# Four partition quarters of the softmax denominators: added through small DMAs and VectorE instead of a product on TensorE

## The chip, the cores and the metric

The kernel runs on one core of one Trainium2 chip. The metric is device time in microseconds (us) of one execution; lower is better. Before the change it is 1316.64 us, the median of three runs (1314.28, 1316.64, 1318.42).

## What is computed

One transformer block in fp32, on an input x of 2 x 512 tokens of width 512, cut to what matters here:

```python
x = x + layernorm(attention(layernorm(x)))   # 32 heads of 128
x = x + layernorm(ffn(layernorm(x)))         # dense base + 8 gated experts of rank 16

# attention, per batch b and head h (64 pairs):
attn = softmax(q[b, h] @ k[b, h].T / sqrt(128))    # 512 x 512
out  = attn @ v[b, h]                              # 512 x 128
# then all heads side by side, 4096 wide:  out @ Wo + bo
```

q and k carry an RMS norm over all 4096 columns and a gain. The change concerns one step of the softmax: the sum of the exponentials of each query, by which the output is divided.

## The kernel before, in words

**Stages.** After the first layer norm the kernel computes q and k (to about 405 us of the profiled span) and then a first part of v; everything is parked in device memory. Products of weights use Winograd's form of 2x2 block products with seven products in place of eight, so that sums of operands are formed on VectorE and GpSimd. From about 450 us to 1232 us runs the **attention loop** (L714 to L762 and the lines after it), and then a tail with the rest of the output product, two layer norms and the feed-forward part.

**The attention loop.** It has N = 64 turns, turn i being head i // 2 of batch i % 2. The order of the instructions on TensorE (PE), VectorE (DVE), ScalarE (ACT) and GpSimd (POOL) is exactly the order in which the program emits them; only the order of the DMAs in the queue of SyncE (SP) is laid out by the framework's scheduler. An engine never runs past an instruction that waits. In turn i:

- DVE: `sums(i - 1)` (L546): the exponentials of the turn before, laid out as keys on partitions and queries along the free axis, are added with a 32x32 block transpose on the way (L550), then over the four blocks of keys (L557). The result, `part`, holds 16 columns for each of 128 partitions: partition 32a + r holds the sum over the a-th quarter of the partitions for query r of each block of 32. So the four quarters still have to be added.
- DVE: `below_top(i)` (L577) subtracts the maximum, 128 x 2048 elements.
- PE: `scores(i + 1)` (L531), four products; ACT copies each out (L532). Then ACT takes the exponential of turn i in one instruction (L580).
- In every even turn: `reciprocals` (L559) for the two turns before. PE multiplies `part` by `same`, a constant 0/1 matrix with a one wherever two partitions are equal modulo 32 (L563). This adds the quarters and leaves the sum in all four. DVE takes the reciprocal from PSUM (L567), and for each of the two turns spreads it out (L570) and multiplies the output with it (`divided`, L598); ACT adds the bias of v (L599).
- PE: the fill. These are steps of v (L460; 1 or 2 a turn up to turn 43, more before turn 8) and tasks of the output product (`through_wo`, L646): group g of eight turns has 14 tasks, and they run in turns 8(g+1) to 8(g+1)+7, for g = 0 to 5. A v step and a task each take 1.72 us of PE. Line L697 deals the tasks out: turns 0 to 7 of a group get 2, 2, 2, 1, 2, 2, 2, 1. From turn 57 on each turn has one `outward` product (L690) of 3.44 us in their place; turn 56 has none.
- DVE: `top_of(i + 1)` (L541, L542) takes the maximum of the next turn's scores over keys, and POOL brings it together over the partitions (L544). Every second turn has two sums of heads on DVE (`head_sums`, L619 to L625), and the turns from 56 on the combining of the output product (L680). Then the results of the fill leave PSUM, through DVE or ACT.
- PE: `weighted(i)` (L589): the product of the exponentials with v. It waits for the exponential of this turn, and for `divided(i - 2)`, because the outputs have two PSUM banks.

Results of v steps, tasks and the product with `same` take turns in three PSUM banks called aux; `bank()` (L515) lets the earlier result leave before a bank is used again. Weights of the output product are loaded by `load_right` (L635) into two buffers.

Of the kernel before, what the change touches and what calls it, by code (L numbers as in the profile page):

```python
# [9 lines left out]
F32 = mybir.dt.float32  # L10
AF = mybir.ActivationFunctionType
ALU = mybir.AluOpType
AX = mybir.AxisListType

P = 128
# [4 lines left out]
NT = S // P  # L20
# [12 lines left out]
def kernel(ctx: ExitStack, tc: tile.TileContext, x, wq, wk, wv, wo, vecs, rows, wbase, gates, bexp, out):  # L33
# [11 lines left out]
    nc = tc.nc  # L45
    B = x.shape[0]
    N = H * B
# [15 lines left out]
    small = ctx.enter_context(tc.tile_pool(name="small", bufs=4))  # L63
# [3 lines left out]
    def tt(name):  # L67
        return tmp.tile([P, 512], F32, tag="tmp", name=name)
# [41 lines left out]
    same = const.tile([P, 4, 32], F32, tag="same", name="same")  # L110
# [196 lines left out]
    def attention():  # L307
# [6 lines left out]
        G = GH * B  # L314
# [23 lines left out]
        WG = NG - 2  # L338
# [52 lines left out]
        for i in range(2):  # L391
            of, to = (v.rearrange("p (g j) -> p g j", j=GH) for v in (vec[:, i, :], steps[:, i, :]))
# [33 lines left out]
        def load_wo(g):  # L426
            wos[g] = []
            for k in range(2):
                w = hpool.tile([P, 2, 512], F32, tag="h", name=f"wo{g}_{k}")
                nc.sync.dma_start(out=w, in_=wo[ts(2 * g + k, 2 * P), :].rearrange("(j p) f -> p j f", p=P))  # L430
                wos[g] += [w[:, j, :] for j in range(2)]
# [60 lines left out]
        def fetch_v(b, c):  # L492

            v = vpool.tile([P, NT, 256], F32, tag="v", name=f"v{b}_{c}")
            src = keptv[b, c // 2].rearrange("t p f -> p t f")
            nc.sync.dma_start(out=v, in_=src[:, :, ts(c % 2, 256)])
            vs[b, c] = v
# [3 lines left out]
        def fetch(i):  # L501
            h, b = divmod(i, B)
            k = kpool.tile([P, 512], F32, tag="k", name=f"kh{b}_{h}")
            nc.sync.dma_start(out=k, in_=keptk[b, h])
            q = qpool.tile([P, 512], F32, tag="q", name=f"qh{b}_{h}")
            nc.sync.dma_start(out=q, in_=keptqs[b, h])
            qs[i], kk[i] = q, k
# [7 lines left out]
        def bank(tag):  # L515
            tile = banks[tag].pop(0)
            banks[tag].append(tile)
            while any(of is tile for of, _ in pending):
                pending.pop(0)[1]()
            return tile  # L520
# [25 lines left out]
        def sums(i, part):  # L546


            quarters = small.tile([P, NT, 16], F32, tag="quarters", name=f"quarters{i}")
            nc.vector.tensor_reduce(  # L550
                quarters.rearrange("p k j -> p (k j)"),
                ss[i].rearrange("p k (j r) -> p (k j) r", r=32),
                AX.X,
                ALU.add,
                apply_transpose=True,
            )
            nc.vector.tensor_reduce(part, quarters.rearrange("p k j -> p j k"), AX.X, ALU.add)  # L557

        def reciprocals(turns, part):  # L559

            n = len(turns)
            psd = bank("aux")[:, 0 : n * 16]
            nc.tensor.matmul(  # L563
                psd, same.rearrange("p i c -> p (i c)"), part.rearrange("p n j -> p (n j)"), start=True, stop=True
            )
            inv = small.tile([P, 2, 16], F32, tag="inv", name=f"inv{turns[0]}")[:, 0:n]
            nc.vector.reciprocal(inv.rearrange("p n j -> p (n j)"), psd)  # L567
            for k, i in enumerate(turns):
                r = tt(f"r{i}")
                nc.vector.transpose(  # L570
                    r.rearrange("p (j c) -> p j c", c=32), inv[:, k].unsqueeze(2).to_broadcast([P, 16, 32])
                )
                yield i, r
# [5 lines left out]
        def exponentials(i):  # L579
            nc.scalar.activation(ss[i], ss[i], AF.Exp)  # L580
# [13 lines left out]
        def divided(i, r):  # L594
            h, b = divmod(i, B)
            po = pos.pop(i)
            o = opool.tile([P, 512], F32, tag="o", name=f"oh{b}_{h}")
            nc.vector.tensor_tensor(o, po, r, ALU.mult)  # L598
            nc.scalar.activation(o, o, AF.Identity, bias=bv[:, h : h + 1], scale=1.0)  # L599
            os[b, h] = o  # L600
            if (b, h % 2) != (1, 0):
                left_of[{(0, 0): 1, (0, 1): 2, (1, 1): 4}[b, h % 2], h // 2] = o
# [28 lines left out]
        def load_right(g, n):  # L631

            w = gpool.tile([P, 2, 512], F32, tag="g", name=f"wr{g}_{n}")
            for half, i in enumerate(product_order[2 * n : 2 * n + 2]):
                k, e = {1: (0, 0), 2: (1, 0), 3: (1, 1), 4: (1, 0), 5: (0, 0), 6: (1, 1), 7: (0, 1)}[i]  # L635
                src = (woq if i <= 3 else keptwo)[g, k]
                nc.sync.dma_start(out=w[:, half, :].rearrange("p (j f) -> p j f", j=2), in_=src[:, :, ts(e, 256)])
                right_of[i, g] = w[:, half, :].rearrange("p (j f) -> p j f", j=2)

        def through_wo(g, i, u):  # L640

            ps = bank("aux").rearrange("p (t e) -> p t e", t=2)
            for t in range(2):
                for j in range(2):
                    a = left_of[i, 2 * g + j][:, ts(2 * u + t, P)]
                    nc.tensor.matmul(ps[:, t, :], a, right_of[i, g][:, j, :], start=(j == 0), stop=(j == 1))  # L646
            to = acc[i][u]

            def add():
                if g > 0:  # L650
                    new = upool.tile([P, 512], F32, tag="u", name=f"w{i}_{g}_{u}").rearrange("p (t e) -> p t e", t=2)
                    nc.scalar.copy(new, ps)
                    nc.gpsimd.dma_start(out=to, in_=new, accum_op=ALU.add)
                elif i in bias_of:
                    nc.vector.tensor_tensor(to, ps, bias_of[i].unsqueeze(1).to_broadcast([P, 2, 256]), ALU.add)
                else:
                    nc.scalar.copy(to, ps)

            return add
# [34 lines left out]
        wo_tasks = {i: [] for i in range(N + 1)}  # L694
        for g in range(WG):
            for k in range(14):
                wo_tasks[G * (g + 1) + k * G // 14].append(  # L697
                    lambda g=g, k=k: through_wo(g, product_order[k // 2], k % 2)
                )
        last = N - G  # L700
# [19 lines left out]
        for i in range(N):  # L720
            g, n = divmod(i, G)
            if i + 3 < N:
                fetch(i + 3)
            c, n4 = divmod(i, 2 * B)
            if 2 <= n4 and 0 < c < H // 2 - 1:
                fetch_v(n4 - 2, c + 1)
            if g >= WG and n == 6:
                load_wo(g)
            if g < WG and n == 7:
                for k in range(2):  # L730
                    load_right(g, k)
            if 0 < g <= WG and n in (2, 4):
                load_right(g - 1, 1 + n // 2)
            if n == 0 and g > WG:
                combining = [step for u in range(2) for step in combined(u)]
            if i % 2 == 1:
                part = small.tile([P, 2, 16], F32, tag="part", name=f"part{i}")
            if i > 0:
                sums(i - 1, part[:, (i - 1) % 2])
            below_top(i)  # L740
            if i + 1 < N:
                scores(i + 1)
            exponentials(i)
            if i > 0 and i % 2 == 0 or i == N - 1:
                turns = (i - 2, i - 1) if i % 2 == 0 else (i - 1,)
                for turn, r in reciprocals(turns, part[:, 0 : len(turns)]):
                    divided(turn, r)
            want = 28 * (i + 1) // G if i < G else 28 + 56 * (i + 1 - G) // (5 * G - 4)
            while left and 84 - left < want:
                leaves(next(v_steps))  # L750
                left -= 1
            for task in wo_tasks[i]:
                leaves(task())
            top_of(i + 1)
            if n4 == 1:
                of_pair = head_sums(c - 1)
            if n4 % 2 == 1 and 0 < c <= 2 * WG:
                next(of_pair)
            for _ in range(3):
                if combining:  # L760
                    combining.pop(0)()
            while len(pending) > (len(wo_tasks[i]) if i >= last else 0):  # L762
                pending.pop(0)[1]()
            weighted(i)
        for task in wo_tasks[N]:
            leaves(task())
        sums(N - 1, part[:, 1])
        while pending:
            pending.pop(0)[1]()
        for turn, r in reciprocals((N - 1,), part[:, 1:2]):  # L770
            divided(turn, r)
        again = [[kpool.tile([P, 512], F32, tag="k", name=f"xr{b}_{t}") for t in range(NT)] for b in range(B)]
        for b in range(B):
# [206 lines left out]
```

## Time and profile before

| what | value |
|---|---|
| median of the runs | 1316.64 us (1314.28 to 1318.42) |
| the profiled execution: time | 1319.28 us |
| the profiled execution: span of the trace | 1317.4 us |
| PE busy | 1284.2 us, 97% of the span |
| DVE busy | 974.4 us, 74% |
| ACT busy | 534.8 us, 41% |
| POOL busy | 483.9 us, 37% |
| products with `same` (L563) | 33 of two passes each |
| granted clock of TensorE | 0.996 of full speed |

How to read it: the span runs from the first to the last instruction of one execution, and the execution's own time is 1.9 us more. The share of busy time is a mean over stages. The views that are used below are the page's groups of instructions (busy time, then mean duration in ns, then the idle time before), the waits (engine and line, what it waited for, total us, times, longest), and the timeline (start, duration, engine, line, operation, and in square brackets the idle time before it and what ended it). PE makes each fp32 product in two passes; an instruction's successor can start before its shown end, so costs are read from starts.

### The profile page before, as it was taken

Reading aid. Unit: us, or ns where it says so; the run is one execution under the profiler, and the core shown is the slowest. Engines: PE = TensorE matmul, PEld = TensorE weight load, DVE = VectorE, ACT = ScalarE, POOL = GpSimd, SP = SyncE. Lnnn points to the kernel's source line nnn. Section 1 sums busy time; section 2 is a strip of 40 time slices with the busy share of each in tenths; the row PEclk is TensorE's granted clock in tenths of the full one; section 3 lists DMA queues with packets and bytes.
Section 4 is the critical chain, followed back from the end, with each engine's and each line's share of the span. In section 5 each row is a group of like instructions: output and inputs, shape, how many; then the busy total and the mean of one; then the engine's idle time right before and its main releaser. Section 6 shows DMA issues by size and latency. Waiting matters only on the chain.

```text
span 1317.4 us, 11573 instructions
## 1 busy us (share of the span) xinstructions
PE 1284.2 (97%) x3470; PEld 643.5 (49%) x3470; DVE 974.4 (74%) x1204; ACT 534.8 (41%) x732; POOL 483.9 (37%) x368
## 2 busy tenths in 40 slices
PE   7999999999989999999999999999999999999997
PEld 4444444444434444455555555555555555434453
DVE  7565654888555468888788787878778888799575
ACT  5222222322221144344545445455454665545253
POOL 4789897565763011111122231322322333221002
PEclk9999999999999999999999999999999999999999
DMA  7789978598897765533366566566567565510001
GB/s 289 263 315 308 338 269 283 193 346 297 304 323 271 251 198 184 176 128 128 128 174 175 138 195 164 132 196 168 159 165 195 129 164 130 136 64 24 18 23 64
DMA packets 146127, 250.45 MB, mean 190 GB/s; under 512 B 11792, under 2 KB 39568, under 8 KB 146064
## 3 DMA queue, kind: packets, MB, share of 16 engines
q1 hardware_dynamic: 135120, 229.78, 51.3%
q0 software_dynamic: 10080, 18.35, 8.5%
q10 hardware_dynamic: 864, 1.57, 0.3%
q8 instruction: 28, 0.46, 0.1%
q14 instruction: 35, 0.29, 0.1%
HBM read 147.43 MB, written 83.89 MB: 176 GB/s over the span
## 4 chain that ended last, share of the span: by engine, by line
PE 64%; DVE 5%; ACT 2%; issue 0%; ACTq 0%; DVEq 0%
PE ps L531 16%; PE o L589 15%; PE aux L460 15%; PE aux L646 11%; PE psy L690 2%; PE p_k L217 2%; PE f L859 1%; ACT s L580 1%; DVE quarters L550 1%; DVE s L577 1%; PE hg L852 1%; PE f L915 1%; DVE m L541 0%; DVE y L680 0%; DVE oh L598 0%
## 5 line engine op out<-in xcount | busy, mean ns | idle before, releaser
L544 POOL PARTITION_ALL_REDUCE top<-m x64 | 122.6, 1916 | 620.7 <-DVE m L542 620.7
L532 ACT ACTIVATE s<-ps,rk 128x512 f32<-128x512 f32 x256 | 175.8, 687 | 312.4 <-PE ps L531 306.8
L589 PE MATMUL o<-s,v 128*128 128x512 f32 x512 | 231.0, 594 | 9.3 <-ACT s L580 9.3
L531 PE MATMUL ps<-qh,kh 128*128 128x512 f32 x512 | 230.2, 592 | 0.0
L531 PEld LDWEIGHTS ps<-qh,kh 128*128 128x128 f32 x512 | 97.3, 190 | 122.5 <-issue 121.7
L589 PEld LDWEIGHTS o<-s,v 128*128 128x128 f32 x512 | 96.6, 190 | 113.4 <-issue 96.4
L550 DVE TRANSPOSE_TENSOR_REDUCE quarters<-s 128x64 f32<-128x2048 f32 x64 | 147.1, 2299 | 0.0
L577 DVE TENSOR_TENSOR s<-s,top 128x2048 f32<-128x2048 f32 x64 | 146.0, 2281 | 0.0
L580 ACT ACTIVATE s<-s 128x2048 f32<-128x2048 f32 x64 | 121.7, 1902 | 12.9 <-DVE s L577 12.8
L541 DVE TENSOR_TENSOR m<-s 128x1024 f32<-128x1024 f32 x64 | 78.0, 1218 | 57.9 <-ACT s L532 57.9
L460 PE MATMUL aux<-w_v,t 128*128 128x512 f32 x256 | 115.8, 596 | 0.0
L237 ACT ACTIVATE sq_q<-q 128x512 f32<-128x512 f32 x62 | 38.9, 631 | 137.0 <-DVE q L290 68.3
L237 ACT ACTIVATE sq_k<-k 128x512 f32<-128x512 f32 x62 | 38.6, 630 | 137.1 <-DVE k L290 64.6
L238 POOL TENSOR_TENSOR accq<-accq,sq_q 128x512 f32<-128x512 f32 x62 | 81.0, 1310 | 36.2 <-ACT sq_q L237 29.3
L238 POOL TENSOR_TENSOR acck<-acck,sq_k 128x512 f32<-128x512 f32 x62 | 86.2, 1395 | 20.3 <-ACT sq_k L237 17.2
L646 PE MATMUL aux<-wr,oh 128*128 128x256 f32 x384 | 88.1, 380 | 0.0
L460 PE MATMUL aux<-w_v,nT_a 128*128 128x512 f32 x192 | 87.5, 596 | 0.0
L217 PE MATMUL p_k<-t,s_k 128*128 128x512 f32 x192 | 85.0, 592 | 0.0
L217 PE MATMUL p_q<-t,s_q 128*128 128x512 f32 x192 | 85.0, 592 | 0.0
L646 PEld LDWEIGHTS aux<-wr,oh 128*128 128x128 f32 x384 | 72.7, 190 | 20.8 <-issue 12.0
L460 PEld LDWEIGHTS aux<-w_v,t 128*128 128x128 f32 x256 | 47.6, 190 | 55.0 <-issue 54.3
L468 DVE TENSOR_TENSOR o_v<-aux,u_v 128x512 f32<-128x512 f32 x64 | 43.5, 684 | 41.4 <-PE aux L460 34.5
(185 smaller groups left out, 1733.8 us busy)
## 6 DMA issues: line engine op xcount, KB each, us to landing
keptq<-q SPq DMA_DIRECT2D x64, 256.0 KB, 7.0
q<-keptq SPq DMA_DIRECT2D x16, 1024.0 KB, 6.7
w_v<-keptw SPq DMA_DIRECT2D x32, 512.0 KB, 3.9
keptk<-k SPq DMA_DIRECT2D x64, 256.0 KB, 6.7
keptqs<-q SPq DMA_DIRECT2D x64, 256.0 KB, 7.0
qh<-keptqs SPq DMA_DIRECT2D x64, 256.0 KB, 2.9
kh<-keptk SPq DMA_DIRECT2D x64, 256.0 KB, 2.7
keptv<-o_v SPq DMA_DIRECT2D x64, 256.0 KB, 3.0
```

The lines of the kernel that those rows point to most:

```text
L217: nc.tensor.matmul(ps, a[:, c, ts(j, P)], x[c], start=(c == 0), stop=(c == 1))
L238: nc.gpsimd.tensor_tensor(accs[b], accs[b], sq, ALU.add)
L460: nc.tensor.matmul(ps, x[c][:, ts(t, P)], w[:, c, :], start=(c == 0), stop=(c == 1))
L531: nc.tensor.matmul(ps, kk[i][:, ts(k, P)], qs[i], start=True, stop=True)
L532: nc.scalar.activation(s[:, k, :], ps, AF.Copy, scale=rks[b][:, k : k + 1])
L541: nc.vector.tensor_tensor(m, s[:, 0:2, :], s[:, 2:4, :], ALU.max)
L544: nc.gpsimd.partition_all_reduce(ms[i], m[:, 0, :], P, ReduceOp.max)
L550: nc.vector.tensor_reduce(quarters.rearrange("p k j -> p (k j)"), ss[i].rearrange("p k (j r) -> p (k j) r", r=32), AX.X, ALU.add, apply_tr ...
L577: nc.vector.tensor_tensor(s, s, top.unsqueeze(1).to_broadcast([P, NT, 512]), ALU.subtract)
L580: nc.scalar.activation(ss[i], ss[i], AF.Exp)
L589: nc.tensor.matmul(po, vs[b, c][:, k, ts(j, P)], ss[i][:, k, :], start=(k == 0), stop=(k == NT - 1))
L646: nc.tensor.matmul(ps[:, t, :], a, right_of[i, g][:, j, :], start=(j == 0), stop=(j == 1))
```

## The change

The product with `same` goes. In its place `spread` (new) copies `part` from SBUF to SBUF on SP's queue, so that each quarter of the partitions gets the sums of the other three beside its own: for each of three rotations two DMAs, since a rotation wraps around, six in all, each of 32, 64 or 96 partitions by 128 bytes. DVE then adds the four (a `tensor_reduce` of 128 x 32 outputs from 128 x 128 inputs) and takes the reciprocal in SBUF.

So that the copies can travel, `reciprocals` and `divided` are emitted later in the turn, after the v steps. The tasks of the output product are dealt out as 0, 2, 2, 2, 2, 2, 2, 2 over the eight turns of a group, and two of its loads are issued one turn later. `part` is larger and has three buffers in place of four; `quarters` has one in place of four. `same` itself stays, for the identity matrix.

```diff
@@ sums
-            quarters = small.tile([P, NT, 16], F32, tag="quarters", name=f"quarters{i}")
+            quarters = small.tile([P, NT, 16], F32, tag="quarters", name=f"quarters{i}", bufs=1)
@@
-        def reciprocals(turns, part):
+        def spread(n, four):
+
+            for k in range(1, 4):
+                for to, of, m in ((0, k, 4 - k), (4 - k, 0, k)):
+                    nc.sync.dma_start(
+                        out=four[32 * to : 32 * (to + m), k, 0:n], in_=four[32 * of : 32 * (of + m), 0, 0:n]
+                    )
+
+        def reciprocals(turns, four):
 
             n = len(turns)
-            psd = bank("aux")[:, 0 : n * 16]
-            nc.tensor.matmul(
-                psd, same.rearrange("p i c -> p (i c)"), part.rearrange("p n j -> p (n j)"), start=True, stop=True
+            inv = small.tile([P, 2, 16], F32, tag="inv", name=f"inv{turns[0]}")[:, 0:n]
+            nc.vector.tensor_reduce(
+                inv.rearrange("p n j -> p (n j)"), four.rearrange("p a n j -> p (n j) a"), AX.X, ALU.add
             )
-            inv = small.tile([P, 2, 16], F32, tag="inv", name=f"inv{turns[0]}")[:, 0:n]
-            nc.vector.reciprocal(inv.rearrange("p n j -> p (n j)"), psd)
+            nc.vector.reciprocal(inv.rearrange("p n j -> p (n j)"), inv.rearrange("p n j -> p (n j)"))
@@ tasks of the output product
-                wo_tasks[G * (g + 1) + k * G // 14].append(
+                wo_tasks[G * (g + 1) + 1 + k // 2].append(
@@ the loop
-            if 0 < g <= WG and n in (2, 4):
-                load_right(g - 1, 1 + n // 2)
+            if 0 < g <= WG and n in (3, 5):
+                load_right(g - 1, (n + 1) // 2)
...
             if i % 2 == 1:
-                part = small.tile([P, 2, 16], F32, tag="part", name=f"part{i}")
+                part = small.tile([P, 4, 2, 16], F32, tag="part", name=f"part{i}", bufs=3)
             if i > 0:
-                sums(i - 1, part[:, (i - 1) % 2])
+                sums(i - 1, part[:, 0, (i - 1) % 2])
+            turns = ()
+            if i > 0 and i % 2 == 0 or i == N - 1:
+                turns = (i - 2, i - 1) if i % 2 == 0 else (i - 1,)
+                spread(len(turns), part)
+                four = part[:, :, 0 : len(turns)]
             below_top(i)
             if i + 1 < N:
                 scores(i + 1)
             exponentials(i)
-            if i > 0 and i % 2 == 0 or i == N - 1:
-                turns = (i - 2, i - 1) if i % 2 == 0 else (i - 1,)
-                for turn, r in reciprocals(turns, part[:, 0 : len(turns)]):
-                    divided(turn, r)
             want = 28 * (i + 1) // G if i < G else 28 + 56 * (i + 1 - G) // (5 * G - 4)
             while left and 84 - left < want:
                 leaves(next(v_steps))
                 left -= 1
+            if turns:
+                for turn, r in reciprocals(turns, four):
+                    divided(turn, r)
             for task in wo_tasks[i]:
                 leaves(task())
@@ after the loop
-        sums(N - 1, part[:, 1])
+        last_part = small.tile([P, 4, 2, 16], F32, tag="part", name="last_part", bufs=3)
+        sums(N - 1, last_part[:, 0, 0])
+        spread(1, last_part)
         while pending:
             pending.pop(0)[1]()
-        for turn, r in reciprocals((N - 1,), part[:, 1:2]):
+        for turn, r in reciprocals((N - 1,), last_part[:, :, 0:1]):
             divided(turn, r)
```

## The prediction

> **What bounds the kernel.** I read the page's busy times first, then the waits, then the timeline of PE and DVE through the attention loop.
>
> ```profile
> PE 1284.2 (97%) x3470; PEld 643.5 (49%) x3470; DVE 974.4 (74%) x1204; ACT 534.8 (41%) x732; POOL 483.9 (37%) x368
> ...
> DVE inv L567 <- PE aux L563: 44.6, 28, 3.9
> ...
> PE o L589 <- ACT s L580: 9.3, 8, 2.4
> ```
>
> PE is the bound. The busy times by stretch show no idle PE at all from 487 to 1010 us (523.00 of 523.00), 2.6 us from 1010 to 1145 and 8.0 us from 1145 to 1232. So in the loop up to turn 46 whatever leaves PE is won, as long as no new wait appears. The second row says that DVE already waits for the product that goes, 28 times, 1.6 us each on average: a DMA wait in its place is no loss until it is longer. The third row is the few waits of PE for the exponential, all from turn 47 on. The timeline of PE shows the price of the product and one of these waits:
>
> ```profile
> 1029.31 3.60 PE L531 MATMUL ps<-qh,kh 128*128 128x512 f32 x8
> 1032.74 3.62 PE L646 MATMUL aux<-wr,s_o 128*128 128x256 f32 x16
> 1036.19 3.60 PE L589 MATMUL o<-s,v 128*128 128x512 f32 x8
> 1039.63 3.60 PE L531 MATMUL ps<-qh,kh 128*128 128x512 f32 x8
> 1043.06 0.30 PE L563 MATMUL aux<-part,same 128*128 128x32 f32 x2
> 1043.20 3.70 PE L646 MATMUL aux<-wr,s_o 128*128 128x256 f32 x16
> 1046.74 3.60 PE L589 MATMUL o<-s,v 128*128 128x512 f32 x8
> 1050.17 3.60 PE L531 MATMUL ps<-qh,kh 128*128 128x512 f32 x8
> 1053.61 1.89 PE L646 MATMUL aux<-wr,s_o 128*128 128x256 f32 x8
> 1056.35 3.70 PE L589 MATMUL o<-s,v 128*128 128x512 f32 x8 [0.85 <-ACT s L580]
> ```
>
> Turns 45, 46 and 47. Without the product, tasks plus scores take 1036.19 - 1029.31 = 6.88; with it 1046.74 - 1039.63 = 7.11. Turn 47 has one task, and PE stands 0.85 for the exponential.
>
> **The product goes.** 0.14 between starts (1043.06 to 1043.20) and 0.09 that the next products take longer (3.54 against 3.45): 0.23 us each. In turns 2 to 54, 27 products at 0.23 = **-6.2**. The six after that stand where PE waits anyway: 0 (bound -1.4). The Trainium skill, "TensorE: Matmul & The Clock Gate", section "Wait — 56ns, not 53.3ns?", puts the floor of a small matmul at about 25 ns from start to start; two passes would be 0.05 and the gain an estimated 1.4 in place of 6.2. These starts disagree, and I go by them.
>
> **The tasks move.** Turns 47, 51 and 55 get a second task, so their waits (0.85, 0.86, 0.86 in the timeline) go: **-2.6**. Turns 8, 16, ... 48 get none. PE needs about 2.8 us between scores and `weighted` to cover copy and exponential (turn 47: 1056.35 - 1053.61 = 2.74). Turns 16, 24 and 40 keep two v steps (3.44): covered. Turn 32 keeps one: it waits like turn 47, 0.86. Turn 48 keeps nothing, like turn 56 today, which waits 2.44. Turn 8 keeps one and is taken up below. The shifted loads keep their two turns of lead: no cost.
>
> **The new wait, D: from the end of `part` to the last copy landed.** No row shows a small copy. SP issues six in a row; kh and qh start 0.38 apart (1063.51, 1063.89), the shortest issue is 0.32, three kh together take 1.44 (0.48 each). I take five steps of 0.40. The smallest landings: 2.0 for a 256 KB store, 2.4 for a 256 KB load (kh), 3.3 for a 512 KB one (v). So 256 KB cost about 0.9, and nothing but overhead is 1.1 (store) or 1.5 (load); I take 1.4, nearer the load since it must be seen in SBUF. D = 2.0 + 1.4 + 0.05 = **3.45**. Ends: 5 x 0.32 + 1.1 = 2.7; 5 x 0.48 + 2.4 = 4.8, and 5.5 if they queue behind other loads. The Trainium skill, "DMA: Bandwidth & Descriptors", section "Anatomy of one DMA — SWDGE (gpsimd) path", gives every DMA about 2.0 us of fixed cost, and its rules for authors advise against transfers under 64 KB. With 2.0 for 1.4 the sum below would rise by an estimated 2 to 3 us, to about no change.
>
> ```profile
> 1058.45 2.30 DVE L550 TRANSPOSE_TENSOR_REDUCE quarters<-s 128x64 f32<-128x2048 f32 x1
> 1060.78 0.26 DVE L557 TENSOR_REDUCE part<-quarters 128x16 f32<-128x64 f32 x1
> 1060.96 2.28 DVE L577 TENSOR_TENSOR s<-s,top 128x2048 f32<-128x2048 f32 x1
> 1063.66 0.36 DVE L567 RECIPROCAL inv<-aux 128x32 f32<-128x32 f32 x1 [0.42 <-PE aux L563]
> 1064.05 0.71 DVE L570 STREAM_TRANSPOSE r<-inv 128x512 f32<-128x512 f32 x1
> 1064.80 0.69 DVE L598 TENSOR_TENSOR oh<-o,r 128x512 f32<-128x512 f32 x1
> ```
>
> Turn 48: `part` ends at 1061.04 and L577 covers 2.2 of D; DVE then waits D - 2.2 = 1.25. The added reduce reads twice L557's elements: 0.26 to 0.36 by L557 and L567, next start about 0.24 later. The reciprocal I leave at 0.39 (PSUM or SBUF, +-0.05). Behind the waiting reduce on DVE stand both transposes, both `divided`, the next maximum (and POOL's after it), and exits of v steps.
>
> *Does DVE become the bound?* From L567 of turn 48 (1063.66) to that of turn 50 (1084.52) DVE idles 1.38 + 1.03, so it works 18.45; after, 18.69 + 1.25 = 19.94. PE needs 6 x 3.44 = 20.64 for the pair. Covered; break-even at D = 2.2 + 20.64 - 18.69 = **4.15**. While v steps run, DVE has 3.8 (turn 12) to 5 us (turn 32) idle a pair: covered to D of about 5.5.
>
> *Turn 8.* `part` ends at 564.35 by the timeline; + 3.45 + 0.24 + 0.39 + 0.75 + 0.69 = 569.87. PE would want `weighted` at 562.63 + 3.43 + 1.72 = 567.78: it waits 2.1 for `divided(6)`. Turn 48: without turn 47's wait `part` ends 0.87 earlier against PE, the same sum gives 5.8 after the scores began, before the exponential (6.1): 2.44 stands. New waits together 2.44 + 0.86 + 2.1 = **+5.4**.
>
> *Turns 56 to 63.* DVE is full here, and PE's waits follow it. DVE waits today at turns 56, 58, 60, 62, 63: 2.47, 0.23, 0, 2.19, 0 = 4.9; after, five times 1.25 + 0.24 = 7.45. +2.5 if all of it counts, 0 if the shorter waits at 56 and 62 give it back into PE's gaps (1.61 in turn 57). I take **+1.0** (ends 0 and +4.5, the three new waits alone).
>
> *SP's queue.* 198 DMAs more at about 0.35. The copies wait at its head for `part`; kh, qh and v behind them are due two or more turns later: 0. The last spread stands behind a load of Wo that waits for PE (1230.24 today), lands near 1234.5, and is needed only by the second half of the final product, after 1245: 0. One-buffer `quarters` stays on one engine: 0.
>
> **Sum:** -6.2 - 2.6 + 5.4 + 1.0 = **-2.4**. The profiled execution (span 1317.4, time 1319.28) would take 1316.9; the median of the runs lies 2.64 lower, so I forecast **1314.2**.
>
> **Rivals.**
> *The copies land sooner (D = 2.7).* For it: bytes are almost none. Turn 8 waits 1.35; turns 56 to 63 have five times 0.74 = 3.7 in place of 4.9, -1.2. Sum -6.2 - 2.6 + 4.65 - 1.2 = -5.3: **1311.3**. Bottom of the range 1308, with the last products' 1.4 and some scatter of the runs.
> *DVE becomes the bound (slower).* Place: turns 46 to 63; decides from D = 4.15. At D = 4.8: five pairs x 0.65 = 3.3; turn 8 +1.35; turn 48 now waits for `divided(46)`, +1.0; the three new waits of the last turns 3 x 1.35 = 4.0. Sum -2.4 + 9.7 = +7.3: **1323.9**. At D = 5.5, +1.35 a pair: about +15, 1332. For it: loads of 256 KB land at 2.7 to 2.9 by the median and DMA is 58% busy; against: in the late loop little is in flight when `part` ends.
> *It doesn't do what it says:* PE loses the products but idles as much. That is the first case with a turn or two more uncovered, within 2 us of no change.
>
> **Chances.** Forecast 0.37, early landing 0.30, DVE bound 0.33. The range 1308 to 1329 reaches into both rivals. About 0.3% (4 us) is what a measurement of this kernel can tell from no change: faster by more 0.31, within 0.36, slower 0.33; the forecast's own range is 1312 to 1319.
>
> **What would show it.** L563 gone, tasks plus scores 6.88 in every turn; PE waits new at 8, 32 and 48 and gone at 47, 51, 55; `part` to reduce 3.45; DVE idle near 1.25 before the reduce. Wrong if a copy's issue or landing is far from 0.40 and 1.4, or if v steps' exits behind the reduce hold PE's banks.

## The result and the profile after

The changed kernel takes **1354.76 us** (median of 4 runs, 1350.44 to 1357.23), the kernel before 1317.53 us on the same chip: ratio **1.0272** [1.0248, 1.0296]. It is 36 us slower. The forecast was 1314.2 with a range of 1308 to 1329, so it is wrong in sign and outside its range. The way it went is the slower rival, *DVE becomes the bound*, but at more than twice the price that the rival had at its far end (+15).

The page of the changed kernel, busy times, then the chain that ended last by engine, then the group of the new reduce (busy, mean ns, idle time before it and what ended that):

```profile
PE 1293.7 (96%) x3404; PEld 639.2 (47%) x3404; DVE 985.6 (73%) x1237; ACT 538.9 (40%) x732; POOL 484.0 (36%) x368
...
PE 63%; DVE 21%; DMA 5%; SPq 4%; issue 3%; ACT 2%; POOL 2%; DVEq 0%; ACTq 0%; POOLq 0%
...
L571 DVE TENSOR_REDUCE inv<-part 128x32 f32<-128x128 f32 (+1 forms) x32 | 12.0, 374 | 103.2 <-DMA part<-part 103.2
```

The chain on the page before:

```profile
PE 64%; DVE 5%; ACT 2%; issue 0%; ACTq 0%; DVEq 0%
```

DVE is busy 73% of the span, as before (74%), so the share of busy time shows nothing. The chain does: DVE has 21% of it where the page before has 5%, and two new members stand beside it, SP's queue (4%) and the DMA of `part` (3%). (The chain before reaches back only to 380 us, so its shares add up to 71%. From turn 1 to turn 63 alone, DVE has 255 of the chain's 781 us after the change, and 56 of 744 before.) The third line of the changed kernel is the cause in one row: DVE stands still 103.2 us ahead of 32 reduces, 3.2 us each, until the copies have landed. Before, it stood 44.6 us for the product in the same place. PE has 66 instructions fewer and is yet busy 9.5 us longer; that is a second effect, taken up below.

The row of the copies and their landing, from the view of the tile `part` (duration of one issue, min/median/max ns; then the time from issue to landing):

```profile
L563 SPq DMA_DIRECT2D part<-part x192: 522/589/1487, 480.5 to 1257.0; - x192
...
DMA to landing us min/median/max: 1.7/1.8/4.6
```

An issue takes 0.59 us by the median where the prediction took 0.40, and a landing 1.8 where it took 1.4. Turn 48 in the timeline of all engines, the same place as the rows of DVE in the prediction:

```profile
1076.14 3.60 PE L531 MATMUL ps<-qh,kh 128*128 128x512 f32 x8
1076.43 0.26 DVE L557 TENSOR_REDUCE part<-quarters 128x16 f32<-128x64 f32 x1
1076.61 2.28 DVE L584 TENSOR_TENSOR s<-s,top 128x2048 f32<-128x2048 f32 x1
1076.72 4.38 SPq L563 DMA_DIRECT2D part<-part  x6
...
1082.56 0.37 DVE L571 TENSOR_REDUCE inv<-part 128x32 f32<-128x128 f32 x1 [3.67 <-DMA part<-part]
1082.96 0.35 DVE L574 RECIPROCAL inv<-inv 128x32 f32<-128x32 f32 x1
...
1084.16 0.69 DVE L605 TENSOR_TENSOR oh<-o,r 128x512 f32<-128x512 f32 x1
...
1084.95 5.37 PE L596 MATMUL o<-s,v 128*128 128x512 f32 x8 [5.21 <-issue]
```

`part` ends at 1076.69. Six issues take 4.38 us, 0.73 each, and the reduce starts at 1082.56: D = 5.87 in place of 3.45. L584 covers the first 2.2, and the remaining 3.67 is DVE's idle time. `weighted` waits for `divided` (L605), so PE stands 5.21 us. Then comes something the prediction had no term for: the same eight passes take 5.37 us, not 3.67.

The busy times by stretch for turns 1 to 8, 8 to 46, 46 to 56 and 56 to 63 (cut at the starts of `weighted`; the columns are the stretch, its length, busy time of PE, PEld, DVE, ACT and POOL, granted clock, DMA share, GB/s). First before:

```profile
481.28:571.46 90.18, 90.18 (x226) 41.94 (x224) 76.60 (x84) 38.60 (x46) 11.29 (x6) 1.00 0.52 174
571.46:1046.74 475.28, 475.28 (x1404) 263.41 (x1402) 379.64 (x383) 236.84 (x298) 118.01 (x91) 1.00 0.57 157
1046.74:1148.30 101.56, 96.56 (x291) 54.04 (x289) 85.96 (x80) 59.69 (x77) 32.93 (x27) 1.00 0.58 150
1148.30:1224.80 76.50, 70.90 (x169) 30.89 (x169) 73.13 (x75) 34.98 (x40) 13.95 (x7) 1.00 0.12 39
sum 743.52, PE 732.92 PEld 390.27 DVE 615.33 ACT 370.11 POOL 176.18; mean PE 183.23 PEld 97.57 DVE 153.83 ACT 92.53 POOL 44.05
```

Then after:

```profile
477.10:567.25 90.15, 85.99 (x201) 37.83 (x200) 75.03 (x84) 37.69 (x44) 11.28 (x6) 0.99 0.55 176
567.25:1062.32 495.07, 482.30 (x1373) 262.07 (x1373) 388.25 (x403) 238.66 (x299) 117.24 (x90) 0.99 0.55 152
1062.32:1172.73 110.41, 99.04 (x288) 54.90 (x289) 88.85 (x87) 62.24 (x79) 33.94 (x28) 0.98 0.57 140
1172.73:1258.10 85.37, 73.68 (x160) 30.97 (x160) 72.82 (x74) 35.25 (x39) 13.95 (x7) 0.96 0.13 40
sum 781.00, PE 741.00 PEld 385.77 DVE 624.95 ACT 373.84 POOL 176.40; mean PE 185.25 PEld 96.44 DVE 156.24 ACT 93.46 POOL 44.10
```

From turn 1 to turn 63 the loop is 781.00 - 743.52 = **37.5 us** longer. By stretch it is 0, +19.8, +8.9 and +8.9: more than half of the loss lies where PE had not idled at all before. By kind: PE's idle time grows from 10.6 to 40.0 (+29.4). Its busy time grows by 8.1, though 32 products went in this stretch (32 x 0.23 = 7.4); so other passes became 15.5 us slower. Six passes of `weighted` (turns 8, 32, 42, 48, 56 and 59) take 4.7 to 6.6 us in place of 3.67 and make 10.8 of that; a seventh, of turn 63, starts where the stretch ends, and with it they make 12.5. Most of the other 4.7 is only how gaps show: PE has 23 gaps here in place of 9, and a pass next to a gap is shown as some 0.25 longer than its step (3.67 or 3.70 for 3.43). That makes 3.5, an estimate.

### The profile page after: what moved, and what is told of

Same layout as the page of the kernel before. It is cut to its first block, busy times and chain, and to the rows that moved or that the text cites. A ratio compares the mean times of both kernels' runs of the same rounds, so it can differ in the third digit from the quotient of the medians.

```text
span 1352.8 us, 11851 instructions
## 1 busy us (share of the span) xinstructions
PE 1293.7 (96%) x3404; PEld 639.2 (47%) x3404; DVE 985.6 (73%) x1237; ACT 538.9 (40%) x732; POOL 484.0 (36%) x368
## 4 chain that ended last, share of the span: by engine, by line
PE 63%; DVE 21%; DMA 5%; SPq 4%; issue 3%; ACT 2%; POOL 2%; DVEq 0%; ACTq 0%; POOLq 0%
PE p_q L217 14%; PE aux L460 10%; PE o L596 10%; PE p_k L217 9%; PE ps L531 9%; PE aux L653 5%; DVE quarters L550 5%; SPq L563 4%; DMA part<-part 3%; DVE m L541 2%; PE psy L697 2%; DMA w_k<-in_wk 2%; DVE oh L605 2%; DVE r L577 2%; DVE s L584 2%
## 5 line engine op out<-in xcount | busy, mean ns | idle before, releaser
L596 PE MATMUL o<-s,v 128*128 128x512 f32 x512 | 244.2, 622 | 32.7 <-ACT s L587 12.3
L596 PEld LDWEIGHTS o<-s,v 128*128 128x128 f32 x512 | 100.3, 199 | 151.1 <-issue 132.1
L584 DVE TENSOR_TENSOR s<-s,top 128x2048 f32<-128x2048 f32 x64 | 146.0, 2281 | 0.0
L571 DVE TENSOR_REDUCE inv<-part 128x32 f32<-128x128 f32 (+1 forms) x32 | 12.0, 374 | 103.2 <-DMA part<-part 103.2
L606 ACT ACTIVATE oh<-oh,vec 128x512 f32<-128x512 f32 x64 | 46.2, 722 | 81.8 <-DVE oh L605 81.7
```

The lines of the kernel that those rows point to most:

```text
L584: nc.vector.tensor_tensor(s, s, top.unsqueeze(1).to_broadcast([P, NT, 512]), ALU.subtract)
L596: nc.tensor.matmul(po, vs[b, c][:, k, ts(j, P)], ss[i][:, k, :], start=(k == 0), stop=(k == NT - 1))
```

## The experiments

Three theories. **T1**: DVE's wait for the copies is the cost, by its length D alone. **R**: the copies cost by their number (traffic, SP's queue). **S**: the new deal of tasks, which leaves turns 8, 32 and 48 uncovered, and the slow passes after them. Each ratio is to the kernel before, run on the same chip, with its 95% interval.

| kernel | copies per pair | median us | ratio |
|---|---|---|---|
| e1_tasks_only | 0 | 1320.90 | 1.0007 [0.9984, 1.0029] |
| e3_copies_unread | 6, unread | 1318.05 | 0.9992 [0.9969, 1.0014] |
| e7_two_copies | 2 | 1314.12 | 0.9973 [0.9953, 0.9993] |
| e10_four_copies | 4 | 1327.90 | 1.0081 [1.0059, 1.0104] |
| the change | 6 | 1354.76 | 1.0272 [1.0248, 1.0296] |
| e2_old_tasks | 6 | 1353.82 | 1.0276 [1.0245, 1.0307] |
| e8_twelve_copies | 6 + 6 unread | 1502.34 (one run) | about 1.14 |
| e4_two_queues | 3 + 3 | 1339.49 | 1.0167 [1.0138, 1.0196] |
| e5_turn_later | 6 a turn | 1315.96 | 0.9982 [0.9964, 1.0000] |
| e9_turn_later_old_tasks | 6 a turn | 1309.82 | 0.9942 [0.9923, 0.9961] |
| e11_filled | 6 | 1361.10 | 1.0337 [1.0308, 1.0367] |
| e12_half_filled | 6 | 1350.20 | 1.0251 [1.0226, 1.0276] |

**One part alone: the tasks (e1).** The kernel before with only the new deal of tasks and the later loads.

```diff
-                wo_tasks[G * (g + 1) + k * G // 14].append(
+                wo_tasks[G * (g + 1) + 1 + k // 2].append(
-            if 0 < g <= WG and n in (2, 4):
-                load_right(g - 1, 1 + n // 2)
+            if 0 < g <= WG and n in (3, 5):
+                load_right(g - 1, (n + 1) // 2)
```

> The kernel before with only the tasks of the output product dealt out as 0, 2, 2, ... and the two loads a turn later; the product with same stays. If the wait for the copies is the cause (T1), this costs little: three waits of 0.86 go, turns 8, 32 and 48 get about 1, 1 and 2.5: 0 to +3 us against before. If the uncovered turns, and the slow passes of PE after them, are the cause (S): +15 us or more. If the copies' traffic is the cause (R): as T1.

Measured: 1.0007 [0.9984, 1.0029], no change that can be told. By itself the deal costs 4 us at the most, where S asked for 15 or more, so S falls as the main cause.

**One part alone: the copies, unread (e3).** The kernel before, with its product, and the six copies beside it into columns that nothing reads.

```diff
+            if i > 0 and i % 2 == 0 or i == N - 1:
+                spread(2 - i % 2, part)
```

> The kernel before, order of tasks and all, with the six copies issued at the place where the changed kernel issues them, into columns that nobody reads; the product with same still gives the sums. T1 (only the wait for the copies costs): within 2 us of before, PE without new waits. R (198 more DMAs in SP's queue and on the DMA engines delay the loads and stores around them): +15 to +35 us, and waits of PE or DVE on kh, v or w_v.

Measured: 0.9992 [0.9969, 1.0014]. The copies are as dear to issue here as in the changed kernel (522/589/1250 ns), and nobody waits: the time stays. R falls. These 192 DMAs in SP's queue cost nothing that can be told (2 us at the most); waiting for them does.

**The opposite undo: old tasks, new copies (e2).** The changed kernel with the two lines of e1 taken back.

> The changed kernel with the old deal of output tasks and the old turns of the loads of Wr; the six copies and the reduce stay. T1 (VectorE's wait of 5.2 to 5.9 us for the copies is the cost, whichever deal): the uncovered turns 8, 32 and 48 get a task back and lose their gaps (4.2, 2.2 and 5.2) and slow passes, but turns 47, 51 and 55 lose theirs in turn: 1350 to 1365, the changed kernel's time within some 5. S (the new deal's uncovered turns and the slow passes after them carry most of the 37 us): 1320 to 1335. R (the traffic of the copies): as the changed kernel, with no shift of gaps between turns.

Measured: 1.0276 [1.0245, 1.0307], the changed kernel's time. PE's gap at turn 8 falls from 4.16 to 0.71 and at turn 48 from 5.21 to 1.64, but turns 9 to 45 now lose 15.7 in place of 11.2, and turns 49 to 55 lose 5.1 in place of 2.7. The deal of tasks mostly says where the wait shows. (In the two traces e2's loop is 5 us shorter, 775.93 us from turn 1 to turn 63 against 781.00; the times don't show it.)

**The dose: two, four, twelve copies (e7, e10, e8).** In e7 one rotation in place of three (the denominators leave out two of the quarters), in e10 two rotations (one quarter is left out); in e8 six copies into unread columns are issued ahead of the six real ones, and `part` has one buffer in place of three.

```diff
-            for k in range(1, 4):
+            for k in (1, 2):           # e10; range(1, 2) in e7
...
-  four.rearrange("p a n j -> p (n j) a"), AX.X, ALU.add
+  four[:, 0:3].rearrange("p a n j -> p (n j) a"), AX.X, ALU.add      # 0:2 in e7
```

> The changed kernel with one rotation in place of three: two copies (96 and 32 partitions), and the reduce adds two quarters, so the denominators leave out two quarters of the keys. Everything else is as changed. T1: the wait D falls from 5.6 to about 0.05 + 0.65 + 1.8 = 2.5, DVE is covered nearly everywhere, and the product's 7.6 us on PE show: 1309 to 1317, that is -7 to 0 against before. R: a third of the traffic leaves a third of the loss: about +12. S: +15 or more.

> The changed kernel with two rotations in place of three: four copies for each pair, and the reduce adds three quarters (one quarter of the partitions' sums is left out of the denominators). D was about 3.6 us with two copies, 5.7 with six and 9.9 with twelve, so four give about 4.5. T1: the time follows D. With the slope between six and twelve copies (148 us for 4.2 us of D) the changed kernel's 37 us above before are 1.05 us of D beyond the break-even, which puts it at 4.65: 1310 to 1325. If instead each copy costs by itself, the line from two copies (3.5 below before) to six (37 above) gives 17 above: 1335.

> The changed kernel with twelve copies for each pair of turns: six more, into columns that nothing reads, are issued ahead of the six that the reduce adds; one buffer of the sums in place of three. T1: six issues at 0.59 to 0.75 each lengthen VectorE's wait by about 3.6 to 4.5, so D goes from 5.7 to 9.5 to 10 us, far beyond the cover, and each of 32 reduces passes nearly all of it on: 1440 to 1500. R (a price for each copy, 1.1 us in all for every six): another 36 us at most, about 1390; the copies unread beside the old product had cost nothing measurable, which speaks against R already.

The row of DVE's waits for the copies (total us, times, longest), first with two:

```profile
DVE inv L571 <- DMA part<-part: 30.9, 32, 3.0
```

With four:

```profile
DVE inv L571 <- DMA part<-part: 62.6, 32, 3.1
```

With twelve:

```profile
DVE inv L572 <- DMA part<-part: 225.5, 32, 7.8
```

The wait follows the number of copies: 1.0, 2.0, 3.2 (six) and 7.0 us for each reduce. From the timelines, the median of D (end of the second sum in `part` to start of the reduce) and the time against before are:

| copies | D, median us | time against before, us |
|---|---|---|
| 2 | 3.02 | -3.6 |
| 4 | 4.07 | +10.7 |
| 6 | 5.33 | +35.8 |
| 12 | 9.18 | +184 |

The slope is 14 us for each us of D between two and four copies, 20 between four and six, 38 between six and twelve. Part of the last slope is slow passes: from turn 1 to turn 63 e8's loop takes 922.38 us in place of 781.00, and PE's busy time in it is 785.12 in place of 741.00. PE's idle time grows by the remaining 97 us, 25 for each us of D: beyond six copies the 32 reduces pass on some four fifths of it as idle time. I expected a sharp knee at D = 4.65 for four copies (1310 to 1325), and a line of equal cost for each copy would have given 1335. Measured is 1327.9, between the two: the knee is soft and lies lower, since the pairs of turns have unequal cover. With two copies the kernel is faster than before, as the prediction's *copies land sooner* said; its sums give -2.4 at D = 3.45 and -5.3 at 2.7, and -3.6 at 3.02 lies between them.

**The price of a copy by itself (e6).** The kernel before, with unread copies in place of e3's: within SBUF (L571: 128 x 128 bytes; L573: 32 x 128 bytes), and from SBUF to device memory (L575: 128 x 128 bytes; L577: 128 x 512 bytes). Each shape has a part of the execution to itself.

> As the unread copies, but of other shapes in each quarter of the loop: three of 128 partitions x 128 bytes, six of 32 partitions x 128 bytes, six of 128 x 128 bytes to device memory, six of 128 x 512 bytes to device memory. If the issue of a small copy is dear because a copy has fewer than 128 partitions, 128 partitions go back to 0.32 to 0.40 us; if because the rows are 128 bytes, only the 512-byte rows do; if because both sides are SBUF, only the copies to device memory do. If it is queueing behind other DMAs, none differs. Time as before within 3 us.

The time is 1318.95 us. The view of line L571, 16 KB within SBUF (an issue's min/median/max ns, then the landing):

```profile
L571 SPq DMA_DIRECT2D part<-part x24: 470/592/602, 482.8 to 663.8; - x24
...
DMA to landing us min/median/max: 1.7/1.8/3.8
```

The view of L573, 4 KB within SBUF:

```profile
L573 SPq DMA_DIRECT2D part<-part x48: 517/588/1108, 686.2 to 867.5; - x48
...
DMA to landing us min/median/max: 1.7/2.2/5.0
```

The view of L575, 16 KB to device memory:

```profile
L575 SPq DMA_DIRECT2D shdram<-part x48: 319/430/1060, 890.8 to 1061.5; - x48
...
DMA to landing us min/median/max: 1.4/2.2/4.4
```

A copy from SBUF to SBUF has an issue of 0.59, whether it moves 16 KB or 4 KB; the same rows to device memory take 0.43, with a minimum of 0.32, which is what the loads of kh take before by the median. The rows of 512 bytes to device memory (L577), which the scheduler laid ahead of the loop, take 0.43 too. So the dear issue goes with both ends in SBUF and not with size. Why the chip does that no run here shows.

**Two queues (e4).** Of each rotation's two copies the second is issued by ACT.

```diff
-                for to, of, m in ((0, k, 4 - k), (4 - k, 0, k)):
-                    nc.sync.dma_start(
+                for queue, to, of, m in ((nc.sync, 0, k, 4 - k), (nc.scalar, 4 - k, 0, k)):
+                    queue.dma_start(
```

> The changed kernel with three of the six copies issued by ACT in place of SP. T1: with three issues on each queue D falls to about 3 x 0.65 + 1.8 + 0.3 = 4.0, below the break-even; but ACT, in order, then waits for the sums of exponentials before it copies the next scores, and TensorE's score products wait for their banks: somewhere between 1312 and 1350, VectorE's idle time ahead of the reduce falling from 103 to some 50 us, and a new wait on ACT showing at the copies of scores.

Measured: 1.0167 [1.0138, 1.0196], as both halves of the expectation had it. D falls to 3.94 by the median and DVE's wait from 103.2 to 61.4 us, which e10 prices at some +11 of the 22 us. What is left goes with the new wait on ACT, which has to see `part` before it copies the next scores. The group of the score products on PE:

```profile
L531 PE MATMUL ps<-qh,kh 128*128 128x512 f32 x512 | 235.5, 597 | 14.7 <-ACT s L532 14.7
```

PE now stands 14.7 us ahead of the scores until ACT has emptied a bank.

**The wait taken away (e5, e9).** Each turn issues its own six copies, and the reduce and the division of turn i - 2 come in turn i, so that a copy has a whole turn to land. e5 keeps the new deal of tasks; e9 has the old one. There are 378 copies in the loop's turns in place of 192, each with one turn's 64 bytes for a partition in place of two turns' 128.

```diff
-            if i > 0 and i % 2 == 0 or i == N - 1:
-                turns = (i - 2, i - 1) if i % 2 == 0 else (i - 1,)
-                spread(len(turns), part)
-                four = part[:, :, 0 : len(turns)]
+            if i > 1:
+                turns, four = (i - 2,), part
+            if i > 0:
+                part = small.tile([P, 4, 1, 16], F32, tag="part", name=f"part{i}", bufs=3)
+                sums(i - 1, part[:, 0, 0])
+                spread(1, part)
```

> Each turn issues its own six copies (384 in all instead of 198 or so), and the reduce, the reciprocal and the division of turn i-2 come in turn i, so that the copies have a whole turn of about 10 to 13 us to land; new deal of tasks. T1 (the wait alone): VectorE no longer idles ahead of the reduce, the product's 7.6 us of TensorE time stay saved, VectorE has one more reduce for each pair (0.24 to 0.38 each, some 0.3 x 32 beside its idle time): 1309 to 1317, 2 to 9 below before. R (cost by the number of copies): above the changed kernel, 1385 or more. S (the uncovered turns 8, 32, 48): 1317 to 1325.

> As the kernel with the division a turn later, but with the old deal of tasks and the old turns of the loads of Wr, so that the turns 8, 32 and 48 keep their tasks. T1: as that kernel within 4, 1309 to 1317. S: 4 to 8 below it. R: 1385 or more.

Measured: 0.9982 [0.9964, 1.0000] and **0.9942 [0.9923, 0.9961]**. Twice the copies (and the same bytes), and 39 and 45 us less than the changed kernel; e9 beats the kernel before by 8 us. Three rows of DVE in e9:

```profile
1060.61 0.26 DVE L557 TENSOR_REDUCE part<-quarters 128x16 f32<-128x64 f32 x1
1060.78 2.29 DVE L584 TENSOR_TENSOR s<-s,top 128x2048 f32<-128x2048 f32 x1
1062.98 0.26 DVE L571 TENSOR_REDUCE inv<-part 128x16 f32<-128x64 f32 x1
```

The reduce follows the subtraction at once and carries no bracket: it adds copies of the turn before. And the rows of PE for turn 46, the turn whose tasks plus scores took 7.11 with the product:

```profile
1039.68 3.60 PE L531 MATMUL ps<-qh,kh 128*128 128x512 f32 x8
1043.11 3.62 PE L653 MATMUL aux<-wr,s_o 128*128 128x256 f32 x16
1046.56 3.60 PE L596 MATMUL o<-s,v 128*128 128x512 f32 x8
```

1046.56 - 1039.68 = 6.88, as the prediction had it. From turn 1 to turn 63 e9's loop is 8.2 us shorter than before: 2.2 of idle time, 7.4 for 32 products, less 1.4 for one slow pass. (The profiled execution of e9 is the longest of its 12 runs, 1317.42 us; some 5 us of that lie ahead of the loop, where turn 1 starts at 486.24 rather than 481.28.) In e5 PE idles 4.6 us more than in e9 (13.0 for 8.4), with slow passes at turns 8 and 48 for e9's one at turn 56: S is real, at about 6 us, once the wait is gone.

**The slow passes (e11, e12).** The changed kernel with unread products ahead of `weighted` in turns 8, 32 and 48.

```diff
+            if i in (8, 32, 48):
+                ps = bank("aux")
+                for k in range(4):      # 8 in e11
+                    nc.tensor.matmul(ps, kk[i + 1][:, ts(k % NT, P)], qs[i + 1], start=True, stop=True)
             weighted(i)
```

> The changed kernel with eight unread products (3.5 us) on TensorE ahead of the weighted passes of turns 8, 32 and 48, which have no task. If the slow passes (6.58, 5.37 and 5.37 in place of 3.67 us) come of TensorE's idle time before them, they fall back to 3.67 and the time falls by up to 6 us, to 1348 to 1352. If they come of something else (the time in the program, or the work done), they stay and the time stays or rises by some us: 1354 to 1362. T1 expects the wait of VectorE in these turns as before.

> As the kernel with filled gaps, with half as many unread products: four calls, which are eight instructions and 3.4 us, ahead of the weighted passes of turns 8, 32 and 48 (eight calls were sixteen instructions and 6.9 us, as long as the gap and the loss of the slow pass together, so that they gained nothing). If the slow passes come of idle time: the passes take 3.6 to 3.7 us, the gaps shrink to about 0.7, 0 and 1.8, and the time is that of the changed kernel less 6, plus 1.3 for turn 32, 1347 to 1352. If they come of the time or the work in the program, they stay, and the time is 1354 to 1358.

e11's time missed: it rose by 6 us instead of falling. Eight fp32 calls are sixteen instructions and 6.9 us, twice what I had written, as long as gap and slow pass together. e12 has half. Turn 8 in the changed kernel:

```profile
561.21 1.88 PE L460 MATMUL aux<-w_v,nT_a 128*128 128x512 f32 x4
567.25 6.58 PE L596 MATMUL o<-s,v 128*128 128x512 f32 x8 [4.16 <-DVE oh L605]
```

And in e12:

```profile
564.97 3.60 PE L778 MATMUL aux<-qh,kh 128*128 128x512 f32 x8
569.29 3.67 PE L596 MATMUL o<-s,v 128*128 128x512 f32 x8 [0.72 <-DVE oh L605]
```

With PE kept at work the passes of turns 8, 32 and 48 take 3.67, 3.60 and 3.67 in place of 6.58, 5.37 and 5.37; in e11 all three take 3.6. So the slow passes come of the idle time before them: that is shown by the passes, and by the granted clock in the last section. By the times alone it isn't, since e12's interval and the changed kernel's overlap; its median lies where it was expected (1350.2 against 1347 to 1352).

## Why the prediction was wrong

The failing step is **D, the new wait**: "I take five steps of 0.40", "I take 1.4", "D = 2.0 + 1.4 + 0.05 = 3.45". It measured 5.33 by the median and 5.02 at the least: beyond the end of 4.8, and near the 5.5 that was given for copies that queue behind loads. In D itself the size failed, not the mechanism. Five steps took 3.4 by the median (3.1 to 3.9) rather than 2.0, six issues 4.0 (3.7 to 4.6), and the landing 1.8 rather than 1.4. The rows it was taken from, loads of kh and qh from device memory, were the wrong ones: a copy inside SBUF costs more to issue. The Trainium skill, "DMA: Bandwidth & Descriptors", section "Anatomy of one DMA — SWDGE (gpsimd) path", gives about 2.0 us of fixed cost on another queue than SP's; the landings here, 1.7 at the least and 1.8 by the median, are nearer to it than the prediction's 1.4. Its advice against small transfers pointed the right way for copies that are waited for, while e3's cost nothing that can be told; the missing 1.4 us of issue is not in that section.

D alone does not make the whole miss. By the prediction's own sums D = 5.5 gives 1332, which is 18 of the 40.6 us between forecast and result. The rest is a second step that failed, the cover taken for granted while v steps run, and a term that the prediction lacked, the slow passes; both are below.

Point by point:

- *The product goes*: right. 0.23 each, 6.88 in place of 7.11, and e9 wins 7.4 for 32 of them. The last six, put at 0, count as well, so the term is -7.4 rather than -6.2.
- *The tasks move*: right by itself. Without the copies, e1's gap at turn 32 is 0.64 (predicted 0.86) and at turn 48 2.43 (2.44), and its time is that of before. With the copies the new waits are larger, because each follows D: turn 8 4.16 for 2.1, turn 32 2.17 for 0.86, turn 48 5.21 for 2.44. 4.16 - 2.1 is what D grew by in turn 8 (from 3.45 to 5.02), within 0.5.
- *Break-even at D = 4.15 in the late loop*: about right. From turn 46's reduce (1059.87) to turn 48's (1082.56) pass 22.69 us, of which DVE is busy 18.54 and waits 3.67 for the copies, against PE's 20.64: DVE is the bound. Turns 48 to 56 take 87.78 in place of 81.31, 1.6 a pair, or 1.2 without the slow pass of turn 48, where the prediction's formula gives 5.5 - 4.15 = 1.35.
- *"While v steps run ... covered to D of about 5.5"*: wrong, and the second largest error. With D at 5.3 the turns 9 to 45 lost 11.2 us of gaps. The prediction added up DVE's idle time in a pair as if it could be used anywhere. Nor was it 3.8 to 5 us in each pair: before the change, DVE idles 26.03 - 23.47 = 2.56 in the pair from turn 6 and 24.29 - 21.17 = 3.12 in that from turn 14. But DVE works in order, and behind the reduce stand the exits of v steps. PE's gaps there are 0.3 to 2.2 us long, and the timeline ends most of them with such an exit (u_v or o_v) that a bank of aux waited for. In e9, without the wait, there is not one gap from turn 1 to turn 46. The prediction named this among what would make it wrong, but gave it no price.
- *The slow passes*: missing altogether, 12.5 us in seven passes. The loop before held no sign of them: its gap of 2.44 at turn 56 is followed by a pass of 3.70. That was luck, as the last section shows.
- *Turns 56 to 63, +1.0*: +8.9 between the passes of these two turns: idle time +6.1 (11.7 for 5.6), two slow passes +3.4, less three or four products.
- *SP's queue and traffic, 0; the last spread, 0*: right (e3; the final product waits 0.32 us, and that for a load of Wo).
- *Reduce 0.24 to 0.36, reciprocal 0.39*: 0.37 and 0.35.
- *The rival, DVE becomes the bound*, foresaw the way with a chance of 0.33; at D = 5.5 it said 1332. It priced the late loop and the uncovered turns, and left out the middle of the loop and the slow passes: 11.2 and 12.5 us, which is about what lies between 1332 and 1354.8.

The step that would have saved the sign: the range of D reached 5.5, and at that end the sum stood at 1332, yet I gave the middle value the forecast, with rows of another kind of transfer under it.

## What to carry to other kernels

Price a DMA on a path by a row with the same two ends, and count the issue of every one of a burst: here six copies of a few KB need 5.3 us, 4 of them for issuing alone. A wait is covered only by work that stands ahead of it on the same engine, not by idle time summed over a stage; look at what is queued behind the waiting instruction. The change pays when the consumer moves to the next turn and the copies get time: twice as many copies, with the same bytes in all, gave -0.6% in e9 in place of +2.7%. And a gap of some 2 us on TensorE can cost 1.7 us more than its length.

## What the runs showed of the hardware

- A copy from SBUF to SBUF took 0.59 us to issue from SP or (0.61) from ACT; to device memory, with the same rows, 0.43, at the least 0.32.
- After some idle stretches of 1.9 us and more TensorE runs at half its clock for a while: passes of 3.67 us took up to 6.7 us (e8), mostly 5.37, 1.7 more. In the stretch from turn 48's to turn 50's reduce, which holds one, the granted clock is 0.93. A finer cut shows that it is 0.50 for 3.41 us, from 0.17 us after the start of `weighted`:

```profile
1059.87:1082.56 22.69, 18.33 (x53) 9.48 (x51) 18.54 (x19) 12.67 (x16) 7.24 (x6) 1.00 0.65 163
1082.56:1106.36 23.80, 21.41 (x60) 11.98 (x61) 18.55 (x18) 11.36 (x14) 5.55 (x4) 0.93 0.34 90
1081.71:1085.12 3.41, 0.17 (x1) 0.20 (x2) 2.39 (x5) 0.79 (x2) 0.00 (x0) 1.00 0.73 260
1085.12:1088.53 3.41, 3.41 (x5) 1.35 (x5) 3.27 (x5) 1.21 (x2) 0.23 (x1) 0.50 0.14 51
```

- Which gap is hit depends on where it lies. In each trace the stretches at half clock start on one grid of 3.41 us steps and last one, two or three of them, and it is PE's busy time within one step that counts. With the 14 traces cut at their grids from turn 1 to turn 63, all 53 steps at full clock with PE busy less than 42% are followed by one at half clock, none of the 3022 with 47% or more is, and of the 11 between them 5 are. So the same gap can go either way. Turn 56 with a gap of 2.44 us in the kernel before, where it falls on two steps:

```profile
1144.18:1147.59 3.41, 1.69 (x6) 0.76 (x4) 1.61 (x3) 3.13 (x5) 0.00 (x0) 1.00 0.49 153
1147.59:1151.01 3.42, 2.71 (x7) 1.27 (x8) 3.35 (x6) 1.99 (x3) 0.00 (x0) 1.00 0.29 103
```

And with 2.43 us in e1, where more of it falls on one (1.32 us busy of 3.42, 39%); there `weighted` takes 5.40:

```profile
1152.92:1156.34 3.42, 1.32 (x3) 0.68 (x4) 3.32 (x6) 3.17 (x4) 0.00 (x0) 1.00 0.58 189
1156.34:1159.75 3.41, 3.41 (x5) 1.35 (x4) 3.34 (x5) 0.21 (x1) 1.92 (x1) 0.50 0.00 0
```

The Trainium skill, "TensorE: Matmul & The Clock Gate", section "Part 1: The HAM clock gate (the "warmup" mystery)", states that the clock falls to half after an idle window of about 3.4 us and comes back after as long a time of work, and that the window runs free. Half the clock for 3.4 us costs an estimated 1.7, which agrees with 5.37 against 3.67. The half clock, the 3.41 us and the grid agree with these traces. That the window has to be idle doesn't: a gap of 1.92 us (e11) within one step was followed by a slow pass, and gaps of 3.44 and 3.74 us (e11), which fall on two steps each, by none.
